# The half tiles of a mixture of experts: which operand stands still in their first matmul

## The chip, the core and the metric

The kernel runs on one core of a Trainium2 chip (trn2), in one launch. The metric is the time of a launch on the device in microseconds, the median of several runs. The profiles are of one execution each, taken by the hardware profiler; its instruction rows name the engine (PE for TensorE's matmuls, PEld for its weight loads, DVE for VectorE, ACT for ScalarE, POOL for GpSimd, SP for the queue that issues most DMAs), and the line of the kernel.

## The reference, cut to what matters

The program is a small hybrid block over 2 x 2048 tokens of 256 numbers, all in f32: a state space layer, a mixture of experts, an attention layer, and the same mixture of experts once more. Each adds its result to its input. The change lies in the experts alone:

```python
scores_BSN = jnp.einsum('bsd,nd->bsn', x, Wr) + br
w_BSN = jax.nn.softmax(scores_BSN, axis=-1)
_, idx_BSK = jax.lax.top_k(scores_BSN + biases_N[None, None, :], K)      # N = 8 experts, K = 2
...
h_NM2H = jnp.einsum('md,ndh->nmh', x_MD, Wl1) + bl1[:, None, :]          # D = 256, 2H = 1024
a_NMH, b_NMH = (h_NM2H[..., :H], h_NM2H[..., H:])
y_NMD = jnp.einsum('nmh,nhd->nmd', jax.nn.silu(a_NMH) * b_NMH, Wl2) + bl2[:, None, :]
...
y_MD = jnp.einsum('mn,nmd->md', ew_MN, y_NMD)
```

Only the two chosen experts of a token have a weight other than zero, so the kernel computes just those: 8192 pairs of a token and an expert.

## The kernel before, in words

Routing (`prepare`, `enter`) puts each pair of token and expert into a slot of a table in DRAM, one region of slots to an expert. The class `Experts` then works through tiles of slots. There are two objects of it: `ffn` (its tiles are named `f` and `fe`), whose late tiles run between the state space layer and the attention layer, and `last` (`g` and `ge`), whose late tiles end the program. The tiles `fe` and `ge` run earlier, among other work.

A full tile has 256 slots of one expert. What is left of an expert's slots after its full tiles fills at most a half tile of 128 slots. `plan` (line 516) lays out the list `self.seq`: full tiles, with five half tiles (NIN = 5) spread evenly among them, and the last tile a full one. Two more half tiles (`self.more`) stand behind a test at run time, `tc.If(beyond > 0)` in line 884, for inputs that need them.

The work on tile i, all in f32:

- `fetch` (line 691): `rows` loads the slots' table rows (`tab`), `load` (line 663) the expert's weights `w1` (1024 KB), `w2` (512 KB) and biases, on SP's queue. `gather` (line 680) brings the tokens' rows into `xs`, by an indirect DMA from POOL.
- `turn` (line 702): TensorE transposes `xs`, ScalarE copies the result to `xT` (features on the partitions, slots along the row).
- `up` (line 735): the product with `w1`, then silu(a) * b, into `gT` (hidden features on the partitions, slots along the row).
- `down` (line 783): TensorE multiplies `gT` by `w2` (line 792), VectorE weighs and adds the bias into `y` (line 805), and POOL issues the scatter that adds `y` to the tokens' rows in DRAM (line 816), one for each 128 slots; a tile's scatters wait for those of the tile before. Between the scatters it issues the gathers of the tile three ahead.

For a full tile `up` calls `up_part` (line 716) for each of four groups of 128 hidden features. There the weights stand still and the 256 slots move: four matmuls (two halves a and b, two steps of the sum over 256 features) write 128 x 512 numbers into one PSUM bank, hidden features already on the partitions. ScalarE computes the Silu with its bias (line 730), VectorE the product (line 731).

For a half tile `up` takes the other way (line 747): the tile's 128 slots, `xT`, stand still, and the weights move, 512 columns at a time, in four matmuls (line 750). The result has the slots on the partitions. ScalarE copies one half of it to SBUF (line 761), VectorE the other (line 759). A second step, `fold` (line 764), turns it: eight transposes of 128 x 128 (line 773), then four Silus (line 778) and four products (line 779).

`run` (line 852) sets the order of a stage. In turn i it does `fetch` for the tile four ahead, `up(i)`, `turn(i + 1)`, `down(i - 1)`, and then `fold(i)`. SP, POOL, ScalarE and VectorE keep the order in which the code is written there; TensorE's order is chosen by the scheduler. The PSUM tags A and B, with two banks each, serve the parts of `up` and the transposes of `fold` in turn; T serves `turn`, C serves `down`.

Of the kernel before, what the change touches and what calls it, by code (L numbers as in the profile page):

```python
# [8 lines left out]
F32 = mybir.dt.float32  # L9
AF = mybir.ActivationFunctionType  # L10
ALU = mybir.AluOpType
AX = mybir.AxisListType

P = 128
DM = 256
KD = DM // P
# [16 lines left out]
NE, FH = 8, 512  # L33
NHT = FH // P
# [12 lines left out]
def kernel(  # L47
# [24 lines left out]
    nc = tc.nc  # L72
# [10 lines left out]
    def bank(tag, name):  # L83
        return ps.tile([P, 512], F32, tag=tag, name=name)
# [26 lines left out]
    ident = const.tile([P, P], F32, name="ident")  # L111
# [168 lines left out]
    class Experts:  # L280
# [454 lines left out]
        def up(self, i, between=None):  # L735
            t = self.ts[i]
            nm = t["nm"]
            pool = fe if i % 2 else self.f2
            t["gT"] = pool.tile([P, NHT, TT], F32, tag="gT", name=f"gT_{nm}", bufs=1)
            if t["nh"] == 2:  # L740
                for j in range(NHT):
                    self.up_part(t, j, "AB"[j % 2])
                    if between is not None and j == 1:
                        between()
                return

            for q in range(2):
                p = bank("AB"[q], f"pab_{nm}_{q}")
                for k in range(KD):
                    nc.tensor.matmul(  # L750
                        p,
                        t["xT"][:, k, :],
                        t["w1"][:, k, q * FH : (q + 1) * FH],
                        start=(k == 0),
                        stop=(k == KD - 1),
                    )
                u = self.f2.tile([P, FH], F32, tag=f"u{q}", name=f"u{q}_{nm}", bufs=1)
                if q:
                    nc.vector.tensor_copy(u, p)
                else:  # L760
                    nc.scalar.copy(u, p)
                t["u", q] = u

        def fold(self, i):
            t = self.ts[i]
            nm = t["nm"]
            if t["nh"] == 2:
                return
            ps2 = []
            for q in range(2):  # L770
                p = bank("AB"[q], f"put_{nm}_{q}")
                for j in range(NHT):
                    nc.tensor.transpose(p[:, j * P : (j + 1) * P], t["u", q][:, j * P : (j + 1) * P], ident)
                ps2.append(p)
            sa = self.f2.tile([P, FH], F32, tag="sh", name=f"sh_{nm}", bufs=1)
            for j in range(NHT):
                c = slice(j * P, (j + 1) * P)
                nc.scalar.activation(sa[:, c], ps2[0][:, c], AF.Silu, bias=t["b1"][:, j : j + 1])
                nc.vector.scalar_tensor_tensor(
                    t["gT"][:, j, :P], ps2[1][:, c], t["b1"][:, NHT + j : NHT + j + 1], sa[:, c], ALU.add, ALU.mult  # L780
                )

        def down(self, i, tag, then):
            t = self.ts.pop(i)
# [67 lines left out]
        def run(self):  # L852
            ahead = 3
            first = next(i for i, t in enumerate(self.seq) if not t[4])
            n = len(self.seq)
            with (
                tc.tile_pool(name=f"f2{self.name}", bufs=2) as self.f2,
                tc.manual_schedule(
                    engines={mybir.EngineType.Pool, mybir.EngineType.Activation, mybir.EngineType.DVE}
                ),  # L860
            ):
                self.fetch(first + ahead + 1, first + ahead)
                self.turn(first)
                assert self.seq[-1][1] == 2
                for i in range(first, n - 1):
                    self.fetch(i + ahead + 2, i + ahead + 1, gather=False)
                    if i == first + 6:
                        with tc.manual_schedule(engines={mybir.EngineType.PE}):
                            beyond = nc.values_load(self.beyond[0:1, 0:1], min_val=0, max_val=NHF - NIN)
                            self.up(i)  # L870
                    else:
                        self.up(i)
                    self.turn(i + 1)
                    if i > first:
                        self.down(i - 1, "C", i + ahead)
                    else:
                        for h in range(2):
                            self.gather(i + ahead, h)
                    self.fold(i)
                    if i == first + 2:  # L880
                        yield
                self.up(n - 1, lambda: self.down(n - 2, "C", None))
                self.down(n - 1, "C", None)
                with tc.If(beyond > 0):
                    for tile in self.more:
                        i = len(self.seq)
                        self.seq.append(tile)
                        self.fetch(i + 1, i + 1)
                        self.turn(i)
                        self.up(i)  # L890
                        self.fold(i)
                        self.down(i, "C", None)

    ffn = Experts("f", tc.dram_tile([NT + TT, DM], F32, name="resid"))
# [3 lines left out]
    with tc.tile_pool(name="ssm1", bufs=1) as s1, tc.tile_pool(name="ssm2", bufs=2) as s2:  # L898
# [315 lines left out]
        for i, (b, s, t) in enumerate(chunks):  # L1214
            j = order.index((b, s)) + 1
# [44 lines left out]
    with tc.tile_pool(name="att1", bufs=1) as a1, tc.tile_pool(name="att2", bufs=2) as a2:  # L1260
# [16 lines left out]
        for k in range(KD):  # L1277
            for c in range(NA):
# [4 lines left out]
                    start=(c == 0),  # L1283
                    stop=(c == NA - 1),
# [285 lines left out]
```

## Time and profile before

| what | us |
|---|---|
| median of 3 runs | 1734.07 (1732.85 to 1741.57) |
| profiled execution, its own time | 1733.28 |
| profiled execution, span from the first to the last instruction | 1731.6 |
| TensorE busy, of the span | 1596.9 |
| stage of the tiles `f`, about | 740 to 910 |
| stage of the tiles `g`, about | 1428 to 1731.6 |
| line 750, half tiles' matmuls, of both stages, records | 40 + 40 |
| line 773, half tiles' transposes, of both stages, records | 40 + 40 |

Times inside the profile are counted from the span's start. The two lines of slices give the shape of the run: 40 slices of 43.3 us, each digit the busy share in tenths, and the tenths of full clock that TensorE was granted.

```profile
PE   6997888989989997999998999899999699999997
PEclk9998998999989998999999999999999899999999
DMA  4111211634435362789852312606463568888882
```

The slices 17 to 20 are the tiles `f`, the slices 33 to 39 the tiles `g`. In a row of the timeline the first number is the start, the second the length of the run of equal instructions (xN of them), and the bracket at the end the idle time before it with what ended it. Matmuls overlap one another and their ends are modelled, so such a length is longer than the time by which the next group follows.

### The profile page before, as it was taken

The numbers are of one execution on the slowest core, as the hardware profiler recorded it, in microseconds if no ns is written. First come the engines' busy times: TensorE is split into PE (matmuls) and PEld (weight loads), VectorE is DVE, ScalarE is ACT, GpSimd is POOL, SyncE is SP. The second block draws the span as 40 slices with busy tenths as digits, with TensorE's granted clock in tenths as the row PEclk, the third lists the DMA queues.
The fourth block names the chain that finished last, engine by engine and source line by source line (L and its number), as shares of the span: only waits on it lengthen the run. The fifth ranks groups of instructions, "written<-read, shape, count | busy, mean of one in ns | idle before, by whom it ended". The sixth has DMA issues, their size and how long they took to land.

```text
span 1731.6 us, 21826 instructions
## 1 busy us (share of the span) xinstructions
PE 1596.9 (92%) x6928; PEld 1182.5 (68%) x6928; DVE 901.2 (52%) x2481; ACT 674.1 (39%) x1348; POOL 734.1 (42%) x702
## 2 busy tenths in 40 slices
PE   6997888989989997999998999899999699999997
PEld 4565555766767775787885575465768588888886
DVE  6778888737557465222237648447554522222222
ACT  4886877856546542222332202001121222333332
POOL 3346456445536565444442003403241543545443
PEclk9998998999989998999999999999999899999999
DMA  4111211634435362789852312606463568888882
GB/s 154 44 69 36 86 62 44 217 99 134 120 65 173 89 176 80 205 255 313 221 114 79 81 42 63 86 14 135 140 124 105 126 184 246 223 230 223 229 212 45
DMA packets 174742, 231.27 MB, mean 134 GB/s; under 512 B 45920, under 2 KB 138080, under 8 KB 174368
## 3 DMA queue, kind: packets, MB, share of 16 engines
q1 hardware_dynamic: 143520, 193.42, 37.8%
q0 software_dynamic: 31104, 36.42, 11.7%
q8 instruction: 56, 0.92, 0.2%
q14 instruction: 62, 0.51, 0.1%
HBM read 192.72 MB, written 37.06 MB: 133 GB/s over the span
## 4 chain that ended last, share of the span: by engine, by line
PE 66%; DMA 11%; DVE 11%; POOL 4%; ACT 3%; issue 3%; another core or an unknown queue 1%; SPq 0%; DVEq 0%; POOLq 0%; ACTq 0%
PE pab_g L722 8%; PE pao L1462 6%; PE pab_fe L722 5%; PE pq L1368 5%; PE pab_f L722 4%; PE pf_g L792 4%; PE pab_ge L722 4%; PE pf_fe L792 3%; PE pvd L1442 3%; DVE xc L1047 3%; PE pk L1368 3%; PE pf_f L792 2%; DMA lb<-sums 2%; PE pi L1143 2%; PE pc L1030 2%
## 5 line engine op out<-in xcount | busy, mean ns | idle before, releaser
L722 PE MATMUL pab_fe<-xT_fe,w_fe 128*128 128x256 f32 x672 | 163.1, 399 | 25.0 <-DVE gT_fe L731 18.5
L722 PEld LDWEIGHTS pab_fe<-xT_fe,w_fe 128*128 128x128 f32 x672 | 132.4, 200 | 53.8 <-DVE gT_fe L731 23.2
L722 PE MATMUL pab_g<-xT_g,w_g 128*128 128x256 f32 x736 | 162.9, 379 | 0.0
L722 PEld LDWEIGHTS pab_g<-xT_g,w_g 128*128 128x128 f32 x736 | 139.4, 190 | 19.1 <-ACT xT_g L713 0.4
L816 POOL DMA_INDIRECT out_dram<-y_g,tab_g x51 | 80.3, 1574 | 141.4 <-DVE y_g L805 62.0
L1368 PE MATMUL pq<-w_qkv_sb,axT 128*128 128x512 f32 x256 | 117.4, 598 | 0.0
L1047 DVE SCALAR_TENSOR_TENSOR xc<-pre,conv_w_sb,xc 128x512 f32<-128x512 f32 x144 | 112.5, 791 | 6.2 <-ACT xc L1039 5.5
L1462 PE MATMUL pao<-w_o_sb,o 128*128 128x256 f32 x512 | 112.0, 380 | 1.3 <-DVE o L1450 1.2
L1462 PEld LDWEIGHTS pao<-w_o_sb,o 128*128 128x128 f32 x512 | 97.0, 190 | 18.1 <-issue 2.9
L731 DVE SCALAR_TENSOR_TENSOR gT_g<-pab_g,b_g,sa_g 128x256 f32<-128x256 f32 x92 | 44.5, 484 | 117.8 <-ACT sa_g L730 107.8
L730 ACT ACTIVATE sa_g<-pab_g,b_g 128x256 f32<-128x256 f32 x92 | 43.6, 474 | 154.4 <-PE pab_g L722 140.9
L433 POOL DMA_INDIRECT table_g<-pay_g,at_g x64 | 62.1, 970 | 88.4 <-DVE w_g L409 55.0
L1030 PE MATMUL pc<-xT,w_in_sb 128*128 128x512 f32 x192 | 94.8, 623 | 0.4 <-ACT xc L1039 0.4
L792 PE MATMUL pf_g<-w_g,gT_g 128*128 128x256 f32 x408 | 92.9, 379 | 0.0
L1084 ACT ACTIVATE lt<-lb,cum 128x128 f32<-128x128 f32 x256 | 82.8, 393 | 21.2 <-DMA lb<-sums 21.2
L731 DVE SCALAR_TENSOR_TENSOR gT_fe<-pab_fe,b_fe,sa_fe 128x256 f32<-128x256 f32 x84 | 39.7, 481 | 95.1 <-ACT sa_fe L730 87.3
L1368 PEld LDWEIGHTS pq<-w_qkv_sb,axT 128*128 128x128 f32 x256 | 48.8, 193 | 58.8 <-issue 57.2
L722 PE MATMUL pab_ge<-xT_ge,w_ge 128*128 128x256 f32 x288 | 68.6, 393 | 17.2 <-ACT xT_ge L713 12.1
L816 POOL DMA_INDIRECT resid<-y_fe,tab_fe x42 | 67.1, 1598 | 35.6 <-DVE y_fe L805 15.2
L792 PE MATMUL pf_fe<-w_fe,gT_fe 128*128 128x256 f32 x336 | 80.6, 394 | 1.4 <-DVE gT_fe L731 1.2
L792 PEld LDWEIGHTS pf_g<-w_g,gT_g 128*128 128x128 f32 x408 | 75.4, 190 | 9.3 <-DVE gT_g L731 0.2
L1383 ACT ACTIVATE kd<-pk 128x512 f32<-128x512 f32 x32 | 19.1, 597 | 158.3 <-PE pk L1368 88.1
(493 smaller groups left out, 3458.5 us busy)
## 6 DMA issues: line engine op xcount, KB each, us to landing
w_g<-in_wl_dram SPq DMA_DIRECT2D x28, 1024.0 KB
w_fe<-in_wl_dram SPq DMA_DIRECT2D x21, 1024.0 KB
lb<-sums SPq DMA_DIRECT2D x32, 512.0 KB
w_f<-in_wl_dram SPq DMA_DIRECT2D x16, 1024.0 KB
o<-prob SPq DMA_DIRECT2D x32, 512.0 KB
w_g<-in_wl_dram SPq DMA_DIRECT2D x28, 512.0 KB
w_fe<-in_wl_dram SPq DMA_DIRECT2D x21, 512.0 KB
w_ge<-in_wl_dram SPq DMA_DIRECT2D x9, 1024.0 KB
```

Source lines behind the costliest of these rows:

```text
L433: i = nc.gpsimd.indirect_dma_start(out=self.table, out_offset=bass.IndirectOffsetOnAxis(ap=at[:, t, c : c + 1], axis=0), in_=pay[:, t, c, ...
L722: nc.tensor.matmul(p[:, q * n : (q + 1) * n], t["w1"][:, k, c * P : (c + 1) * P], t["xT"][:, k, :], start=(k == 0), stop=(k == KD - 1),)
L730: nc.scalar.activation(sa[:, :n], p[:, 0:n], AF.Silu, bias=t["b1"][:, i : i + 1])
L731: nc.vector.scalar_tensor_tensor(t["gT"][:, i, :n], p[:, n : 2 * n], t["b1"][:, NHT + i : NHT + i + 1], sa[:, :n], ALU.add, ALU.mult)
L792: nc.tensor.matmul(pos[h][:, h * DM : (h + 1) * DM], t["gT"][:, j, h * P : (h + 1) * P], t["w2"][:, j, :], start=(j == 0), stop=(j == NHT ...
L816: j = nc.gpsimd.indirect_dma_start(out=self.acc if self.direct else self.acc[: self.seq[i][4] or NT + TT, :], out_offset=bass.IndirectOffs ...
L1030: nc.tensor.matmul(pc, w_in_sb[:, k, DI + c * P : DI + (c + 1) * P], xT[:, k, :], start=(k == 0), stop=(k == KD - 1),)
L1047: nc.vector.scalar_tensor_tensor(xc[:, c, :], pre[:, c, j : j + TG], conv_w_sb[:, c, j : j + 1], xc[:, c, :], ALU.mult, ALU.add,)
L1084: nc.scalar.activation(lt[:, i, :], lb[:, i, :], AF.Relu, bias=g["cum"][:, t, i : i + 1], scale=-1.0)
L1368: nc.tensor.matmul(p, src[:, k, t * P : (t + 1) * P], w_qkv_sb[:, k, j, half * TG : (half + 1) * TG], start=(k == 0), stop=(k == KD - 1),)
L1442: nc.tensor.matmul(pvd, w_qkv_sb[:, k, 2, c * P : (c + 1) * P], xd[:, k, :], start=(k == 0), stop=(k == KD - 1),)
L1462: nc.tensor.matmul(po[:, j * DM : (j + 1) * DM], o[i][:, c, (t + j) * P : (t + j + 1) * P], w_o_sb[:, c, :], start=(c == 0), stop=(c == NA ...
```

## The change

Half tiles are worked in the form of full tiles: `up` calls `up_part` four times for them too, with 128 slots in place of 256. The weights stand still, the slots move, and the hidden features come out on the partitions. The branch for half tiles in `up`, the step `fold`, its two calls and the buffers `u0`, `u1` and `sh` are gone. `up_part` itself is as it was: for a half tile its n is 128, so that a part fills half of its bank, and the Silu and the product take 128 x 128 numbers. The diff, whole but for context:

```diff
@@ up @@
             t["gT"] = pool.tile([P, NHT, TT], F32, tag="gT", name=f"gT_{nm}", bufs=1)
-            if t["nh"] == 2:
-                for j in range(NHT):
-                    self.up_part(t, j, "AB"[j % 2])
-                    if between is not None and j == 1:
-                        between()
-                return
-
-            for q in range(2):
-                p = bank("AB"[q], f"pab_{nm}_{q}")
-                for k in range(KD):
-                    nc.tensor.matmul(
-                        p,
-                        t["xT"][:, k, :],
-                        t["w1"][:, k, q * FH : (q + 1) * FH],
-                        start=(k == 0),
-                        stop=(k == KD - 1),
-                    )
-                u = self.f2.tile([P, FH], F32, tag=f"u{q}", name=f"u{q}_{nm}", bufs=1)
-                if q:
-                    nc.vector.tensor_copy(u, p)
-                else:
-                    nc.scalar.copy(u, p)
-                t["u", q] = u
-
-        def fold(self, i):
-            t = self.ts[i]
-            nm = t["nm"]
-            if t["nh"] == 2:
-                return
-            ps2 = []
-            for q in range(2):
-                p = bank("AB"[q], f"put_{nm}_{q}")
-                for j in range(NHT):
-                    nc.tensor.transpose(p[:, j * P : (j + 1) * P], t["u", q][:, j * P : (j + 1) * P], ident)
-                ps2.append(p)
-            sa = self.f2.tile([P, FH], F32, tag="sh", name=f"sh_{nm}", bufs=1)
             for j in range(NHT):
-                c = slice(j * P, (j + 1) * P)
-                nc.scalar.activation(sa[:, c], ps2[0][:, c], AF.Silu, bias=t["b1"][:, j : j + 1])
-                nc.vector.scalar_tensor_tensor(
-                    t["gT"][:, j, :P], ps2[1][:, c], t["b1"][:, NHT + j : NHT + j + 1], sa[:, c], ALU.add, ALU.mult
-                )
+                self.up_part(t, j, "AB"[j % 2])
+                if between is not None and j == 1:
+                    between()
@@ run @@
                         for h in range(2):
                             self.gather(i + ahead, h)
-                    self.fold(i)
                     if i == first + 2:
                         yield
...
                         self.up(i)
-                        self.fold(i)
                         self.down(i, "C", None)
```

## The prediction

> **What bounds the kernel.** I read the page's parts 1 and 4 first, then a table of windows over the two stages in which the experts' half tiles run, then the timeline of TensorE around half tiles, then the stretches in which TensorE stood still.
>
> ```profile
> PE 1596.9 (92%) x6928; PEld 1182.5 (68%) x6928; DVE 901.2 (52%) x2481; ACT 674.1 (39%) x1348; POOL 734.1 (42%) x702
> PE 66%; DMA 11%; DVE 11%; POOL 4%; ACT 3%; issue 3%; another core or an unknown queue 1%; SPq 0%; DVEq 0%; POOLq 0%; ACTq 0%
> ```
>
> TensorE carries most of the chain. What counts is whether it does so where the half tiles are. The rows of line 773 have 40 records in stage f (from 778.4 us) and 40 in stage g (from 1487.8 us), 8 to a tile, so five half tiles run in each stage; the spare ones behind the `If` do not run. Windows (columns: PE, PEld, DVE, ACT, POOL busy, granted clock, DMA share, GB/s):
>
> ```profile
> 800.00:830.00 30.00, 27.70 (x123) 22.64 (x122) 7.48 (x18) 8.93 (x21) 14.01 (x12) 0.94 0.95 285
> 830.00:860.00 30.00, 30.00 (x140) 24.61 (x139) 8.46 (x20) 8.92 (x21) 12.91 (x10) 1.00 0.81 217
> 1478.00:1528.00 50.00, 50.00 (x239) 42.55 (x238) 13.72 (x31) 15.95 (x37) 24.36 (x19) 1.00 0.82 224
> 1528.00:1578.00 50.00, 50.00 (x238) 42.58 (x237) 13.55 (x30) 15.59 (x36) 23.32 (x18) 1.00 0.81 219
> ```
>
> Stage g and the later part of stage f are TensorE without a gap at clock 1.00; DVE and ACT are under a third busy and the DMA engines have a fifth free. Only around 800 us is there a hole. One half tile in g, on TensorE:
>
> ```profile
> 1480.66 3.60 PE L750 MATMUL pab_g<-w_g,xT_g 128*128 128x512 f32 x8
> 1484.10 0.60 PE L709 MATMUL pxs_g<-ident,xs_g 128*128 128x128 f32 x4
> 1484.53 3.62 PE L792 MATMUL pf_g<-w_g,gT_g 128*128 128x256 f32 x16
> 1487.99 1.04 PE L773 MATMUL put_g<-ident,u_g 128*128 128x128 f32 x8
> ```
>
> Each group starts before the printed end of the one ahead, so the cost of a group is the distance of starts, not its printed length. `up` costs 1484.10 - 1480.66, by the start times 3.433 us (8 records 429 ns apart: each of the 4 matmuls of the code leaves two records); `fold`'s transposes 0.873 us (8 records 109 ns apart, up to 1488.86, where the next tile's line 722 begins).
>
> **What the change takes out and puts in.** Per half tile, on TensorE:
> - out: 3.433 + 0.873 = 4.306 us.
> - in: four `up_part`, each 4 matmuls of 128x128 weights against 128 slots, so 16 matmuls and 32 records, each with its own weight load.
>
> The distance of those 32 records decides the case, and no row of the half tile shows it. Two rows are near, at full clock:
>
> ```profile
> 266.72 0.61 PE L1103 MATMUL pb<-xc 128*128 128x128 f32 x4
> 1342.65 1.62 PE L330 MATMUL pr_g<-wr_sb,rxT_g 128*128 128x8 f32 x14
> ```
>
> Line 1103 has the very form: two f32 matmuls with 128 moving columns, four records, a new weight load for each. Their starts lie 112, 112 and 111 ns apart, and the next instruction follows after 112. Line 330 moves only 8 columns and still has 111 to 112 ns, so 112 ns is what a weight load costs back to back, and 128 moving columns hide under it. The full tiles' 256 columns take 216 ns and 512 columns take 429, so 128 columns alone would need about 109. I take 112: 32 x 0.112 = 3.584 us. Saved: 4.306 - 3.584 = 0.722 us a half tile. Bounds: 109 ns (the moving columns alone, as the transposes have) gives 0.82 us saved; 125 ns (an estimate for a partial collision of weight load and moving data over 32 records, where line 1103 shows only four) gives 0.31.
>
> Here the Trainium skill, TensorE: Matmul & The Clock Gate, section LDWEIGHTS (loading the stationary operand), would give less: a weight load takes its columns divided by 1.2 GHz, 107 ns for 128. By that rule 3.41 us, 0.89 saved a tile, 8.9 us over ten. The measured 112 stands nearer to this kernel, so the rule serves only for the lower end of the range. A rule of the same page speaks against the change: Why this matters for your kernels warns that thin matmuls (M under 512) let the clock gate swing unless they run without a pause. At half the clock the 32 records would take about twice 3.58 us, and ten tiles would cost 29 us more than before. The trace shows no such thing: the window 524 to 546 us holds line 1143's streams (64 moving columns, 112 ns apart) at clock 1.00. The dip that it does show, at 805.7 us, follows 2.3 us of standing still. I leave the clock as it is.
>
> Other engines, per half tile: ACT loses its copy of 0.585 us, DVE its copy of 0.692; the four Silus (367 ns) and the four products (345 ns) stay, moved from `fold` up into `up`. ACT now has the Silus ahead of the copy of the next tile's xT. A part takes TensorE 8 x 0.112 = 0.90 us, so ACT follows; its last Silu ends about 3.58 + 0.17 + 0.37 = 4.1 us after the tile's start, just when the transposes of line 709 are done (3.58 + 0.44 + 0.17). The copy (0.59) ends near 4.8, and the next `up` wants it at 3.58 + 0.44 + 3.46 = 7.5. So nothing is late, with 2.7 us of cover. On DVE the products stand ahead of y of the tile before, which waits for line 792 until about 7.4 us. Banks: before, a half tile took two banks for the product and two for the transposes, now four for the parts, in the same A, B rotation; all were emptied some 4 us earlier. gT is ready about 4 us earlier than before, and `down` of the half tile comes a whole tile later, so that gains nothing. In the built program the order on SP and POOL is the same line for line, and TensorE differs in these groups only: no DMA is moved past another. ACT and DVE wait four times for TensorE where they waited twice, behind nothing that is wanted.
>
> **Where the saving can get lost.** The second half tile of f runs into the hole:
>
> ```profile
> 799.29 3.60 PE L750 MATMUL pab_f<-w_f,xT_f 128*128 128x512 f32 x8
> 802.72 0.27 PE L709 MATMUL pxs_f<-ident,xs_f 128*128 128x128 f32 x1
> 805.30 0.55 PE L709 MATMUL pxs_f<-ident,xs_f 128*128 128x128 f32 x3 [2.30 <-DMA xs_f<-xnd_f,tab_f]
> 805.68 5.31 PE L792 MATMUL pf_f<-w_f,gT_f 128*128 128x256 f32 x16
> ```
>
> ```profile
> 797.30 1.56 POOL L816 DMA_INDIRECT resid<-y_f,tab_f  x1 [6.71 <-DVE gT_f L731]
> 799.16 1.00 POOL L683 DMA_INDIRECT xs_f<-xnd_f,tab_f  x1 [0.30 <-issue]
> ```
>
> TensorE waits there for rows gathered by an instruction that stands on POOL behind a scatter. y of that scatter's tile was done at 789.3 us, so the named DVE is not the cause: POOL waited for the scatter before it (issued 787.71) to land, while the 4 MB of the attention weights, issued at 780.8, held the DMA engines. None of that hangs on TensorE's pace after 779 us. So the gather lands at 805.3 as before, and what the first half tile saves (0.722) and what the second pays ahead of the hole (3.584 - 3.433 = 0.151) go into the wait, which grows to about 2.9 us. Behind it the second still drops its transposes: 0.873. The other three give 3 x 0.722 = 2.166. Stage f: 3.04 us.
>
> Stage g: five half tiles at 0.722 = 3.61 us. Weights there are asked for three tiles (some 30 us) ahead; the DMA share would go from 0.82 to about 0.83 as 49.4 us a round become 48.7. The end follows TensorE: the last scatters start at 1720.93 and 1722.78, behind y (1718.95 and 1720.69) and behind the landing of the scatter ahead (issued 1716.33), which hangs on TensorE in the same way; they move with it. The stretch between f and g begins with a load that waits for f's last scatter, and shifts as a whole.
>
> Sum: 3.04 + 3.61 = 6.65 us off the profiled execution's own time of 1733.28, so 1726.6; the median of the three runs is 0.8 above that execution, so I say 1727.4 (0.38% less). What this measurement can tell from no change is about 0.5%, 8.7 us, and the sum stays below it.
>
> **Rivals.**
> - Likeliest (0.72): 4 to 8.6 us gained, about 1727.4.
> - The saving is eaten (0.10): TensorE, once faster, waits for gathers or weights in other rounds too. For it: DMA share 0.81 to 0.95 and POOL's waits for landed scatters. Against it: no wait of TensorE for a DMA in g behind 1431 us, and gathers issued two tiles ahead. Half or more of 6.65 would go: 1731 to 1734.
> - The weight load is not hidden (0.06), the case on the other side. Its printed length is 190 ns (line 722), and a printed matmul of 128 columns is 273; if 32 loads in a row ran at 190 ns, a tile would take 6.08 us, 1.77 more, and ten tiles 17.7: about 1752. It decides from 4.306 / 32 = 135 ns upward, and passes 0.5% at 162 ns. Lines 1103, 330 and 1143 all speak against it.
> - More than reckoned (0.12): 107 to 109 ns a record, or the clock dip after the hole (3.4 us at half clock, 1.7 us lost) falls elsewhere: 1723.5 to 1726.
>
> The change does what it says: the transposes and copies go, so that is no rival. The range takes in 125 ns a record (about 3 us gained) and one more dip of the clock at its upper end, 107 ns and no dip at its lower: 1723.5 to 1732.0. Chances: faster 0.16 (the last rival and the likeliest's edge), same 0.78, slower 0.06.
>
> **What would show it.** Right: 32 records of line 722 with 128x128 tiles 112 ns apart; a round in g of 48.7 us for 49.4; the hole before 805.3 us at about 2.9 us; clock 1.00 in g. Wrong: records at 135 ns or more, a clock below 1.00 behind half tiles, or new waits of line 709 for xs_g.

## The result and the profile after

| | before | after |
|---|---|---|
| median, us (22 runs each, same chip) | 1735.27 (1728.1 to 1743.5) | 1731.04 (1725.03 to 1736.83) |
| ratio, 95% interval | | 0.9975 (0.9963 to 0.9987) |
| profiled execution, its own time / its span | 1733.28 / 1731.6 | 1731.15 / 1729.5 |

The ratio means 4.3 us less, with an interval of 2.3 to 6.4. The forecast was 6.65 us less and 1727.4 us, from the first three runs of before. The time lies inside the range and the sign is right; the gain came out at two thirds. Of the 3.6 us by which 1731.04 lies above 1727.4, 1.2 are the median of before, which rose from 1734.07 with more runs, and 2.4 the smaller gain. Single executions of before alone spread over 15 us, so the time inside the range says little of the mechanism; that is read from the traces. Two later measurements of the same kernel (below) gave 10.6 and 4.2 us.

In the profile after, the line numbers of `down` are 38 lower: its matmuls are line 754, its `y` line 767, the scatter line 778. First the page's busy row:

```profile
PE 1596.3 (92%) x7088; PEld 1199.9 (69%) x7088; DVE 896.7 (52%) x2471; ACT 672.2 (39%) x1338; POOL 736.1 (43%) x702
```

TensorE has 160 records more (10 tiles, 32 for 16), DVE and ACT 10 fewer each. The busy time of TensorE is nearly the same, 1596.3 for 1596.9: printed lengths overlap, so the gain is not to be read from this row. Three windows of the two stages (columns: PE, PEld, DVE, ACT, POOL busy, granted clock, DMA share, GB/s):

```profile
800.00:830.00 30.00, 27.53 (x141) 24.18 (x140) 7.50 (x17) 8.68 (x20) 13.12 (x11) 0.94 0.94 287
830.00:860.00 30.00, 30.00 (x165) 26.98 (x164) 8.25 (x19) 8.67 (x20) 14.67 (x12) 1.00 0.87 231
1478.00:1528.00 50.00, 50.00 (x258) 44.47 (x257) 13.25 (x30) 15.80 (x37) 24.03 (x19) 1.00 0.86 230
```

Clock 1.00 and no gap in g, as before. The same half tile of g on TensorE, with the next tile's first row to close it:

```profile
1482.13 3.73 PE L722 MATMUL pab_g<-xT_g,w_g 128*128 128x128 f32 x32
1485.70 0.60 PE L709 MATMUL pxs_g<-ident,xs_g 128*128 128x128 f32 x4
1486.13 3.62 PE L754 MATMUL pf_g<-w_g,gT_g 128*128 128x256 f32 x16
1489.59 7.07 PE L722 MATMUL pab_g<-xT_g,w_g 128*128 128x256 f32 x32
```

From the stream's start to the transposes' is 3.57 us, where the old form took 3.433 and, three rows on, 0.873 more. Behind line 754 the next tile starts at once. From this half tile of g to the next (1530.84) is 48.71 us, for 49.46 before. ScalarE and then VectorE in the same place:

```profile
1485.90 0.37 ACT L730 ACTIVATE sa_g<-pab_g,b_g 128x128 f32<-128x128 f32 x1 [0.53 <-DVE gT_g L731]
1486.34 0.59 ACT L713 COPY xT_g<-pxs_g 128x512 f32<-128x512 f32 x1
```

```profile
1486.30 0.35 DVE L731 SCALAR_TENSOR_TENSOR gT_g<-pab_g,b_g,sa_g 128x128 f32<-128x128 f32 x1 [0.54 <-ACT sa_g L730]
1489.86 0.88 DVE L767 SCALAR_TENSOR_TENSOR y_g<-pf_g,tab_g,by_g 128x256 f32<-128x256 f32 x2 [3.21 <-PE pf_g L754]
```

The copy of the next xT ends at 1486.9, 2.7 us before line 722 wants it; VectorE's products are long done when y comes. The hole in stage f, the stretch in which TensorE stands still for gathered rows, is still there:

```profile
796.69 0.41 PE L709 MATMUL pxs_f<-ident,xs_f 128*128 128x128 f32 x2 [0.69 <-DMA xs_f<-xnd_f,tab_f]
800.39 3.73 PE L722 MATMUL pab_f<-xT_f,w_f 128*128 128x128 f32 x32
803.96 0.27 PE L709 MATMUL pxs_f<-ident,xs_f 128*128 128x128 f32 x1
806.71 0.55 PE L709 MATMUL pxs_f<-ident,xs_f 128*128 128x128 f32 x3 [2.47 <-DMA xs_f<-xnd_f,tab_f]
807.09 5.31 PE L754 MATMUL pf_f<-w_f,gT_f 128*128 128x256 f32 x16
```

```profile
798.26 1.56 POOL L778 DMA_INDIRECT resid<-y_f,tab_f  x1 [7.72 <-issue]
800.13 1.01 POOL L683 DMA_INDIRECT xs_f<-xnd_f,tab_f  x1 [0.30 <-issue]
```

Again the gather stands behind a scatter ahead of which POOL sat idle for 7.7 us, and line 754 behind the hole takes 5.31 us for 3.62, at half clock. The wait of the hole is 2.47 us, not the 2.87 of the forecast; but TensorE now also waits 0.69 us one turn earlier, where it did not wait before. Together that is 3.16 us for 2.30.

To set the executions side by side I use three stretches of TensorE, all by the starts in the traces: f from its first record of line 722 to its last matmul with w2, g likewise, and what lies between. The net length of f leaves out what is lost in waits and at half clock: the time by which a start comes later than is usual for its form (112, 216 or 429 ns).

| us | before | after |
|---|---|---|
| f | 153.63 | 150.83 |
| f, net / lost in waits and half clock | 149.21 / 4.42 | 145.52 / 5.31 |
| f's end to g's start | 533.95 | 537.10 |
| g | 279.06 | 275.37 |

f and g together gave 6.49 us (2.80 and 3.69; the forecast had 3.04 and 3.61), which is the sum of the forecast to within 0.2. But the profiled span shrank by 2.1 only: the stretches that the change does not touch were 1.1 us (ahead of f) and 3.15 us (between f and g) longer in this execution. Whether that is chance or a cost was the open question.

### The profile page after: what moved, and what is told of

Same layout as the page of the kernel before. It is cut to its first block, busy times and chain, and to the rows that moved or that the text cites. A ratio compares the mean times of both kernels' runs of the same rounds, so it can differ in the third digit from the quotient of the medians.

```text
span 1729.5 us, 22154 instructions
## 1 busy us (share of the span) xinstructions
PE 1596.3 (92%) x7088; PEld 1199.9 (69%) x7088; DVE 896.7 (52%) x2471; ACT 672.2 (39%) x1338; POOL 736.1 (43%) x702
## 4 chain that ended last, share of the span: by engine, by line
PE 64%; DVE 11%; DMA 10%; POOL 6%; issue 3%; ACT 3%; SPq 1%; another core or an unknown queue 1%; DVEq 0%; POOLq 0%; ACTq 0%
PE pab_g L722 9%; PE pao L1422 6%; PE pab_fe L722 5%; PE pq L1328 5%; PE pab_f L722 5%; PE pf_g L754 4%; PE pab_ge L722 3%; PE pf_fe L754 3%; DVE xc L1007 3%; PE pk L1328 3%; PE pvd L1402 2%; PE pi L1103 2%; DMA lb<-sums 2%; PE pc L990 2%; PE pf_f L754 2%
## 5 line engine op out<-in xcount | busy, mean ns | idle before, releaser
L722 PE MATMUL pab_g<-xT_g,w_g 128*128 128x256 f32 (+1 forms) x896 | 181.5, 361 | 0.0
L722 PEld LDWEIGHTS pab_g<-xT_g,w_g 128*128 128x128 f32 x896 | 158.4, 190 | 19.6 <-ACT xT_g L713 0.4
L730 ACT ACTIVATE sa_g<-pab_g,b_g 128x256 f32<-128x256 f32 (+1 forms) x112 | 51.0, 455 | 191.2 <-PE pab_g L722 170.3
L731 DVE SCALAR_TENSOR_TENSOR gT_g<-pab_g,b_g,sa_g 128x256 f32<-128x256 f32 (+1 forms) x112 | 51.5, 460 | 129.0 <-ACT sa_g L730 119.8
L722 PE MATMUL pab_f<-xT_f,w_f 128*128 128x256 f32 (+1 forms) x512 | 96.6, 346 | 0.0
L722 PEld LDWEIGHTS pab_f<-xT_f,w_f 128*128 128x128 f32 x512 | 85.4, 191 | 9.4
L722 PE MATMUL pab_ge<-xT_ge,w_ge 128*128 128x256 f32 x288 | 69.9, 399 | 19.5 <-ACT xT_ge L713 14.2
```

What stands on the lines that cost most here:

```text
L722: nc.tensor.matmul(p[:, q * n : (q + 1) * n], t["w1"][:, k, c * P : (c + 1) * P], t["xT"][:, k, :], start=(k == 0), stop=(k == KD - 1),)
L730: nc.scalar.activation(sa[:, :n], p[:, 0:n], AF.Silu, bias=t["b1"][:, i : i + 1])
L731: nc.vector.scalar_tensor_tensor(t["gT"][:, i, :n], p[:, n : 2 * n], t["b1"][:, NHT + i : NHT + i + 1], sa[:, :n], ALU.add, ALU.mult)
```

## The experiments

My theory: TensorE carries both stages, a half tile saves what its streams save, and only the wait near 805 us takes part of it back; the rest of the difference is the spread of executions. Rival 1: what f saves is given back between f and g. Rival 2: waits for rows and weights eat the saving. The kernel before ran beside the others in every set of runs. Its median went from 1731 to 1743 us from one set to another, and those two sets were on the same chip, so only ratios within a set are compared.

**One stage alone.** The old branch and `fold` stay for one of the two stages; here for g alone, and the mirror image (`not self.direct`) for f:

```diff
 # before.py, in up and in fold
-            if t["nh"] == 2:
+            if t["nh"] == 2 or self.direct:
```

> The new form for half tiles in stage g alone; stage f keeps the old form with its transposes. Theory (TensorE carries both stages, and a half tile saves 0.735 us wherever TensorE does not stand still): g, from its first matmul of line 722 to its last of w2, goes from 279.1 to 275.4 us, f stays at about 153.6; the launch is 3.7 us shorter than before. Rival (the saving is eaten by waits for rows and weights): g shrinks by less than 2 us, and lines of TensorE's idle time before xs_g appear. Rival (only f pays): nothing is gained.

> The new form in stage f alone. Theory: f goes from 153.6 to about 150.7 us (five half tiles at 0.735, less what one and a bit lose in the wait for gathered rows near 805 us), g stays at 279.1; the launch is 2.9 us shorter than before. Rival (what f saves is given back between f and g, where the profile of the changed kernel is 3 us longer than the one of before): f's stage shrinks alike, but the stretch from f's last to g's first matmul grows by 2 to 3 us and the launch is within 1 us of before.

g alone: ratio 0.9976 (0.996 to 0.9992), 4.2 us less; g 275.37 us, f net 149.21. f alone: 0.9995 (0.9981 to 1.0009), 0.9 us less, anywhere from 3.3 less to 1.6 more; f net 145.52, g 279.06. So each stage shows its 3.69 us of TensorE work gone exactly where the new form is, and g's reaches the end. For f the interval holds the theory's 2.9 and the rival's nothing alike. The two gains add up to 5.1 us. The hole in these two executions, first with f's old form, then with its new one:

```profile
804.80 3.60 PE L750 MATMUL pab_f<-w_f,xT_f 128*128 128x512 f32 x8
808.24 0.27 PE L709 MATMUL pxs_f<-ident,xs_f 128*128 128x128 f32 x1
809.70 0.55 PE L709 MATMUL pxs_f<-ident,xs_f 128*128 128x128 f32 x3 [1.19 <-DMA xs_f<-xnd_f,tab_f]
```

```profile
806.51 3.73 PE L722 MATMUL pab_f<-xT_f,w_f 128*128 128x128 f32 x32
810.09 0.27 PE L709 MATMUL pxs_f<-ident,xs_f 128*128 128x128 f32 x1
812.86 0.55 PE L709 MATMUL pxs_f<-ident,xs_f 128*128 128x128 f32 x3 [2.50 <-DMA xs_f<-xnd_f,tab_f]
```

The idle time in the brackets is 1.19 and 2.50 us here and was 2.30 in the kernel before: the hole is no fixed quantity. In neither of these two did the half clock follow it.

**The attention weights' loads, moved.** In the kernel after and in the one before:

```diff
-                    if i == first + 2:
+                    if i == first + 8:
                         yield
```

> The changed kernel, with the two loads of the attention weights (4 MB) issued six tiles later in stage f, at the tile that starts near 831 us. Theory (these loads hold up the scatters and through them POOL's gather, which makes TensorE stand still near 805 us): the wait of 2.5 us for xs_f and the stretch of half clock behind it (1.7 us) go, so f takes about 146 to 147 us in place of 150.8, and nothing as large takes its place; the launch is about 11 us shorter than before. Rival (the gather is late by POOL's own order of scatters and gathers): the wait near 805 us stays at over 2 us. Rival (the jam only moves): a wait of 2 us or more for xs_f shows up near 850 us.

> The kernel before, with the same move of the two loads. Theory: f goes from 153.6 to about 150 us (2.3 us of waiting and 1.7 us of half clock), the launch is 4 us shorter than before; and the gap to the changed kernel with the loads moved is 5 x 0.735 = 3.7 us in f, where with the loads in their old place it is 2.8. Rival (the wait does not take up what half tiles save): the gap in f is 2.8 in both.

After with the move: 0.9975 (0.9957 to 0.9994); before with it: 1.0 (0.9979 to 1.0021). The wait near 805 us went, and one near 872 us came:

```profile
871.90 0.27 PE L709 MATMUL pxs_f<-ident,xs_f 128*128 128x128 f32 x1
874.18 0.55 PE L709 MATMUL pxs_f<-ident,xs_f 128*128 128x128 f32 x3 [2.02 <-DMA xs_f<-xnd_f,tab_f]
```

f took 150.59 and 153.15 us, nearly its old lengths, with 5.07 and 3.95 us lost. The theory of both runs, that the hole would go, fell; the rival that the jam moves along held. The gap between the two is 3.69 us net and 2.56 in length, nearer to the rival's 2.8 than to the theory's 3.7; since a hole stayed in both, the pair could not show what f gives without one.

**The changed kernel again.**

> The changed kernel once more, beside the three kernels below on one chip. Theory (both stages pay in full, less what the wait near 805 us takes): 6.6 us shorter than before. Rival (only g's 3.7 us reach the end): 3 to 4.5 us shorter, as the 22 runs of the result have it (4.2).

Ratio 0.9939 (0.9918 to 0.9961), 10.6 us less (6.8 to 14.2); f 150.36 us (4.84 of it lost), g 275.37. More than forecast, where the first measurement had less. The two intervals (0.9963 to 0.9987 and 0.9918 to 0.9961) do not meet, so the ratio moves from one set of runs to another by more than an interval of one set tells.

**Half tiles' matmuls made twice,** in f alone (`not self.direct`) and in g alone:

```diff
-            for q, c in ((0, i), (1, NHT + i)):
+            twice = 2 if t["nh"] == 1 and self.direct else 1
+            for q, c in ((0, i), (1, NHT + i)) * twice:
```

> The changed kernel with the 16 matmuls of each half tile in stage f made twice, into the same banks (the second pass clears and rewrites them): 5 x 3.57 = 17.9 us more of TensorE in f. Theory (TensorE's time in f passes on to the end, one for one): f's net length goes from 145.5 to 163.4 us, less up to 3 us that the wait for gathered rows gives back, and the launch is 15 to 18 us longer than the changed kernel, 9 to 12 longer than before. Rival (something between f and g hangs on another clock than f's end): the stretch from f's last to g's first matmul shrinks, and the launch is less than 10 us longer than the changed kernel, under 5 longer than before.

> The same doubling in stage g alone. Theory: g goes from 275.4 to 293.2 us, with no wait of TensorE in it, and the launch is 17.9 us longer than the changed kernel, 11 to 13 longer than before. Rival (waits in g take up part of it): g under 290 us.

g: 293.24 us, 17.87 more than with single streams, and the ratio to before is 1.0062 (1.0039 to 1.0085), 10.8 us more. f: 1.0064 (1.0043 to 1.0085), 11.1 us more; against the changed kernel on the same chip the medians differ by 20.7 us (f doubled) and 19.5 (g doubled). Forecast were 15 to 18 and 17.9 us. So time in f does pass on to the end, and the rival that something between f and g does not hang on f's end, which allowed under 5 us more than before, falls. In the profiled execution of the doubled f the hole is gone:

```profile
807.68 7.31 PE L723 MATMUL pab_f<-xT_f,w_f 128*128 128x128 f32 x64
814.82 0.60 PE L709 MATMUL pxs_f<-ident,xs_f 128*128 128x128 f32 x4
815.26 3.62 PE L755 MATMUL pf_f<-w_f,gT_f 128*128 128x256 f32 x16
```

The 64 records go straight into four transposes. f is 163.43 us long with 0.06 lost, in place of some 4.6. Counted from f's first line 722, the gather is issued at 45.6 us (before), 45.5 (after) and 46.8 (f doubled), while TensorE reaches that turn at 49.2, 49.3 and 55.5. The rows come at a time that TensorE's pace hardly moves: a slower TensorE meets them landed, a faster one waits. All seven profiles with the loads in their old place and no doubling in f agree: counted in the same way, TensorE goes on behind the hole at 51.8 and 50.5 us with the old form (before, g alone) and at 51.3 to 52.3 us with the new one (five profiles), so not earlier, though its work ahead of the hole is 0.6 us shorter; these times scatter by more than that.

The launch does not show this give-back. Both doublings add the same work, and only f's lost its wait, so f doubled should end some 4.5 us ahead of g doubled (0.06 us lost in f for a mean of 4.56, below); its median is 1.2 us behind, with an interval of about 4 us on either side of each. The profiled execution was also the fastest of its six, 1738.03 us where the other five took 1744.4 to 1746.8. What the wait is worth in the launch is thus not shown.

**The loads behind the last tile's weights** (`first + 12` in place of `first + 2`).

> The changed kernel with the loads of the attention weights behind the last tile's weights, near 877 us of the profile. Moved by six tiles the jam moved with them, so: theory (the loads themselves make the gathers late, wherever they stand): no wait of TensorE for xs_f in the middle of f, at most one at the last tile, f at 145.5 to 147 us, and the launch 3 to 5 us shorter than the changed kernel. Rival (4 MB do not land by f's end): TensorE waits for w_qkv_sb behind f, and the launch is no shorter than the changed kernel.

Ratio 0.9969 (0.9956 to 0.9982); the median is 4.0 us above that of the changed kernel beside it, where 3 to 5 us less were expected. f took 153.06 us, 7.54 of them lost, for the 145.5 to 147 of the theory: the rival's wait for the attention weights behind f did not come, and the middle of f is free of waits, but the turn behind its last half tile pays:

```profile
890.77 3.73 PE L722 MATMUL pab_f<-xT_f,w_f 128*128 128x128 f32 x32
896.23 0.30 PE L709 MATMUL pxs_f<-ident,xs_f 128*128 128x128 f32 x1 [1.73 <-DMA xs_f<-xnd_f,tab_f]
900.00 0.90 PE L709 MATMUL pxs_f<-ident,xs_f 128*128 128x128 f32 x3 [3.47 <-DMA xs_f<-xnd_f,tab_f]
```

**The loads in eight pieces of 512 KB,** one behind each tile's own weights:

```diff
-                    if i == first + 2:
+                    if i >= first + 2:
                         yield
...
-    next(late)
-    nc.sync.dma_start(w_qkv_sb.rearrange("p k j e -> p k (j e)"), w_qkv.rearrange("(k p) e -> p k e", p=P))
-    nc.sync.dma_start(w_o_sb, w_o.rearrange("(k p) d -> p k d", p=P))
+    pieces = [(w_qkv_sb[:, k, j, :], w_qkv[k * P : (k + 1) * P, j * AW : (j + 1) * AW]) for k in range(KD) for j in range(3)]
+    pieces += [(w_o_sb[:, c : c + 4, :], w_o[c * P : (c + 4) * P, :].rearrange("(k p) d -> p k d", p=P)) for c in (0, 4)]
     for _ in late:
-        pass
+        if pieces:
+            nc.sync.dma_start(*pieces.pop(0))
```

> The changed kernel with the 4 MB of attention weights cut into eight loads of 512 KB, one behind the weights of each tile from the third of stage f on. Theory (the wait of TensorE in f is the jam behind one 4 MB block, wherever the block stands): no wait for xs_f over 1 us and no stretch of half clock, f at 145.5 to 147 us against 150.4 to 151.1, the launch 4 to 5 us shorter than the changed kernel and about 11 shorter than before. Rival (any added traffic in f makes a gather late): waits of 2 us or more remain, f over 149 us.

> The kernel before with the same spread loads. Theory: f at its net length, 149.2 us, 3.7 longer than the changed kernel's with spread loads: without the wait all five half tiles pay; the launch about 3.5 to 4.5 us shorter than before. Rival: f over 152 us, a wait remains.

After with pieces: 0.9966 (0.9941 to 0.999), before with pieces: 0.9987 (0.9967 to 1.0006). f took 153.30 us in both, with 7.77 and 4.09 us lost:

```profile
842.82 0.27 PE L709 MATMUL pxs_f<-ident,xs_f 128*128 128x128 f32 x1
847.89 0.90 PE L709 MATMUL pxs_f<-ident,xs_f 128*128 128x128 f32 x3 [4.80 <-DMA xs_f<-xnd_f,tab_f]
```

The theory fell, the rival held: the loads leave a gather late even in small pieces. In every one of these profiles but the doubled f it is the turn behind a half tile that waits longest, and there the second half of the rows: one transpose runs and three stand. That turn is of the tile four ahead of an earlier half tile, and `down` of a half tile issues the second gather behind that half tile's scatter (line 826 of the kernel before), which waits for the scatter of the tile ahead of it. No version beats the change itself beyond its interval.

This order on POOL alone does not make the hole. The turn behind the third half tile of f in the kernel before stands in the same order, after the loads:

```profile
825.40 1.00 POOL L683 DMA_INDIRECT xs_f<-xnd_f,tab_f  x1 [0.31 <-issue]
834.78 0.60 PE L709 MATMUL pxs_f<-ident,xs_f 128*128 128x128 f32 x4
```

Its gather is issued 9.4 us ahead of TensorE (8.3 at the fourth, 854.33 and 862.64), and TensorE does not wait; at the hole the gather has 3.6 us. No run leaves the loads out, but with them moved by six tiles the second half tile's turn is free of waits and the fourth's has the hole.

**The changed kernel a third time,** beside the last two.

> The changed kernel a third time, on the chip of this call. Theory: 6.6 us shorter than before (ratio 0.996); the two measurements so far are 4.3 and 10.6 us shorter with intervals that barely meet. Rival (only g's 3.7 us reach the end): 0.998.

Ratio 0.9976 (0.9955 to 0.9998), 4.2 us less; f 149.67 us (4.15 lost), g 275.37.

**Fewer slots moved.** Only 64 of a half tile's 128 columns go through `up`; the other 64 get their results.

```diff
-                        p[:, q * n : (q + 1) * n],
+                        p[:, q * n : q * n + w],
...
-                        t["xT"][:, k, :],
+                        t["xT"][:, k, :w],
```

Here w is 64 for a half tile; its Silu takes 64 columns, and its product is written twice.

> The changed kernel with only 64 of a half tile's 128 slots moved through the up matmuls; the other 64 slots get the same results, so half of these tiles' slots are left out of the computation. Theory (at 128 columns the weight loads set the pace of 112 ns): the 32 records of a half tile stay 111 to 112 ns apart, g stays at 275.4 us. Rival (the moved columns set it): they come 55 to 60 ns apart, and g is 8 us shorter.

One execution. TensorE on a half tile of g:

```profile
1478.44 3.68 PE L723 MATMUL pab_g<-xT_g,w_g 128*128 128x64 f32 x32
1481.95 0.61 PE L709 MATMUL pxs_g<-ident,xs_g 128*128 128x128 f32 x4
```

32 records still take 3.51 us, 111 to 112 ns each but for the first (55); g is 275.14 us, and the rival's 8 us less are out. Half the moved columns leave the pace as it is, so the columns do not set it. Each record has a weight load of its own; that this load sets the pace is what is left, and fits the 112 ns of line 330 with 8 columns.

## Why the prediction was right, and where it was off

- **The distance of the 32 records.** Taken at 112 ns from line 1103; every half tile has 111 to 112 (109 for the first), 3.571 us a tile for the 3.584 of the sum. A tile saved 0.735 where 0.722 was forecast. The rival with 190 ns and the bound of 125 are out.
- **The clock and the transposes.** In the profile after, the clock was 1.00 in g, and in f but for 3.4 us at the hole. The swing of thin matmuls, of which the Trainium skill warns (TensorE: Matmul & The Clock Gate, Why this matters for your kernels), did not come in these unbroken streams. The next tile starts where line 773 stood.
- **Stage g.** Forecast 3.61, measured 3.69, and the same in each execution: all eight profiles with g's new form as in the change have 275.37, all four with the old form 279.06. No wait inside.
- **The other engines.** The copy of xT ended with the 2.7 us of cover that the sum gave it.
- **The hole in f: landing right, size open.** The forecast held the landing of the gather fixed and let the wait grow by 0.57 us (to 2.87), with 3.04 left of f's saving. The landing did stay, to within 1.8 us (50.5 to 52.3 us behind f's start in these seven profiles), but the lost time did not all go into that wait: in the profile after, 0.69 us of it stand one turn earlier. That pair of profiles has 2.80 us left of f's saving. In the profiles with the loads in their old place the new form lost 5.31, 2.91, 4.84, 4.15 and 5.58 us in f (after, f alone, the two repeats, g doubled; mean 4.56), the old form 4.42 and 1.46 (mean 2.94). That is 1.6 us more, so that f pays about 3.69 - 1.6 = 2.1. Whether the half clock follows the wait decides some 1.6 us of each of these figures, and only two profiles have the old form, so the 2.1 is an estimate and does not rule out 3.04. The trace of the doubled f shows the wait give way to TensorE's pace; its launch does not show the gain.
- **The hole's cause.** The forecast named the 4 MB of attention weights. The wait follows them, and turns in the same order away from them do not wait, or by 1 us at most, so they have a part in it; but it comes back wherever they are put, whole or in pieces, and each time at the turn behind a half tile. So that cause was too narrow: the place in POOL's queue belongs to it. How much of a scatter's long landing is due to the loads and how much to the scatters' own order was not told apart.
- **The sum.** 2.1 + 3.69 = 5.8 us. The three measurements of the change, 0.9975, 0.9939 and 0.9976, weighted by the inverse square of their intervals' widths, give 0.9968, or 5.5 us. Their widths alone give about 1.6 us to either side, and since two of them do not meet it is more. So 5.5 fits 5.8 and the forecast's 6.65 alike, and its closeness to 5.8 is in part luck. The 3.15 us that the first profile lost between f and g did not come back as a rule: f doubled passed on at least what its trace has. That stretch, and the one ahead of f, vary more than the change is worth (in all profiles here the attention's output product, from its first to its last matmul, runs over 319 to 329 us). Rival 1 is thus excluded as a general law; a give-back of a microsecond could not be seen.

## What to carry to other kernels

For a product of small tiles compare the distance of starts, not printed lengths, for both ways of placing the operands, and count what the second way saves behind it: here 8 wide records plus 8 transposes (4.31 us) against 32 narrow ones (3.57 us), with the narrow ones at a pace that their moved columns do not set. A saving in a stage whose engine has no gaps arrived in full here; where the engine already waits for a transfer that comes at its own time, what is saved ahead of the wait goes into it. Before moving a load away from such a wait, see whether another gather, as late in its queue, takes over.

## What the runs showed of the hardware

In f32 a stream of 128x128 weight loads, each with its own matmul, runs at 112 ns a record with 64 moving columns and with 128 alike (3.51 and 3.57 us for 32), though a load is printed with 190 ns and a matmul of 128 columns with 272; 256 columns take 216. Transposes of 128x128, whose loads are printed with 140 ns, come every 109 ns. And the length of a wait alone does not tell whether half clock follows: 3.4 us of it followed a wait of 2.30 us of TensorE (before) and of 2.47 us (after), none one of 2.50 (f alone).
